# A two-layer recurrence-and-experts kernel: layer 0's router with stationary weights and ScalarE sums of squares, and three shared-expert tiles placed behind the routed experts

## The chip, the cores and the metric

The kernel runs on one core of one Trainium2 chip. Its time is device microseconds of that core, taken over several executions; beside these times there is one execution recorded by the hardware profiler, with a time and a span of its own. All data are f32. The core has a TensorE (matrix products and transposes, with a sequencer for its weight loads), a VectorE, a ScalarE, a GpSimd and a SyncE (SP) that issues most DMAs; PSUM, where TensorE writes, is used here in banks of 128 partitions by 512 f32.

## The reference

`x` and the side input `k` are (4, 512, 512) and `cond` is (4, 128). Two layers are added to `x` one after the other. Each layer runs a recurrence over the tokens and then a mixture of experts on what comes out:

```python
def bi_wkv(r, k, v, w, u, time_emb):              # called with v = k
    tf = sigmoid(sum(time_emb, -1))
    decay = exp(-exp(w)) * (0.5 + 0.5 * tf)
    ek = exp(min(k, 30)); ekv = ek * v
    # a = a*decay + ekv_t, b = b*decay + ek_t, scanned forward (nf, df) and backward (nb, db)
    euk = exp(min(u + k, 30))
    num = nf + nb - ekv + euk * v
    den = df + db - ek + euk
    return sigmoid(r) * (num / max(den, 1e-8)) * (0.8 + 0.2 * tf)

def ffn0(z):          # 8 experts, 2 per token, 256 wide, one shared expert 256 wide
    h = z * rsqrt(mean(z * z) + 1e-6) * rms_weight
    top2 of softmax(h @ router_w), renormalised to sum 1
    return sum_top2 w_e * ((silu(h @ gate_e) * (h @ up_e)) @ down_e) \
           + (silu(h @ sw_gate) * (h @ sw_up)) @ sw_down

def ffn1(z):          # 32 experts, 6 per token, capacity 512, 352 wide, a shared expert 704 wide
    ...

x = x + ffn0(bi_wkv(x, k, k, w0, u0, cond))
x = x + ffn1(bi_wkv(x, k, k, w1, u1, cond))
```

The change concerns `ffn0` alone: the mean of `z * z`, the product with `router_w`, and the shared expert.

## The kernel before, in words

The 2048 tokens are 16 row tiles of 128 (`NT`), in four blocks of four (`NB`, `TB`; a block is one sequence of the batch). The 512 channels are four chunks of 128 (`NC`). Layer 0's recurrence output lies transposed in `zT`: channels on partitions, tokens along the free axis. A unit is one (block, chunk), `zcols(n)` its 128 x 512 part of `zT`; there are 16 units.

**Recurrence.** A loop over n = 0 to 16 works on several units at once, with the order on ScalarE, TensorE and VectorE written out by hand as it stands in the code. In round n TensorE sums the parts of numerator and denominator of unit n-1 (`sums`, L436 and L437, into banks `num` and `den`), ScalarE turns the denominator into a reciprocal with Ln and Exp, `front(n+1)` and `turn(n+3)` prepare later units (`turn` transposes `k`, L394, from `kr`, which SP loads), `mid(n)` holds the scans on VectorE, and `back(n-1)` multiplies the result into `zT`. `sigmoids` (L465) puts sigmoid(x) there first, once for each block.

**Routing of a block.** It runs in the rounds after the block's last unit: `logits0` in the round with chunk 1, then `route_v` (mean square to 1/rms: a VectorE multiply-add, then Ln and Exp on ScalarE), and `route_max`, `route_top`, `route_pay` in the round with chunk 2, `route_pos` and `route_slots` in that with chunk 3. The last block's routing stands behind the loop; I call these four pieces of work the routing quarters (n = 5, 9, 13 and the last). `logits0` holds two groups of 16 products, each product with eight columns of result in bank `pl`: on L481 a 128-token piece of `zT` is the stationary operand and the chunk's `rout` (128 x 8) moves; on L490 a piece of the squared columns is stationary and a column block of ones moves, which sums squares over channels. The squared columns come from `square(n-2)`, one ScalarE activation per unit into one of four buffers with tag `sq`. `row_tile(n-5)` transposes one row tile of `zT` per round back to rows in a bank `tr`, ScalarE copies it to `zr` (L472), and SP stores it to `z0d` in DRAM (L473), from where the routed experts gather their tokens.

**Shared expert of layer 0.** For a row tile t there are six steps: `share_up` (16 products, L579, gate into one half and up into the other half of one PSUM bank `g`), `share_silu` (ScalarE, L584), `share_hid` (VectorE), `share_turn` (two transposes, L596, and a ScalarE copy), `share_down` (two products in four passes, L605) and `share_add` (VectorE adds to the `x` rows in `acc`; SP stores the tile to `xa`, L610). Tiles 0 to 5 are done in pairs inside the loop, at n = 7, 10 and 13. Tiles 6 to 15 follow the last routing quarter as "the tail". `scale_weights` multiplies `rout` and the shared gate and up weights by `rms_weight` on ScalarE (L243) in round 2.

**Routed experts of layer 0.** `routed` walks over eight experts and their slots of 128 tokens, as many as the counts ask for: 35 slots in the profile. For each slot GpSimd gathers 128 rows from `z0d` by an indirect DMA (L763), TensorE transposes them into `pza` (L776), ScalarE copies them with the scale of `rms_weight` to `zgT`, and TensorE makes gate (L826, into bank `pgate0`) and up (L830, into bank `pup0`). ScalarE runs Silu on gate (L833), then `copy_hidden` for the previous slot's transposed hidden row (L795), then scales up (`upt`, L836); GpSimd multiplies both (`hrow`, L837). TensorE makes the down-projection of the previous slot (L804, into one of two banks `pout`), ScalarE copies it (`ob`, L806), and GpSimd adds it by an indirect scatter (L809), in turn to `xa` and to `xb` (which GpSimd set to zero at the start). Weights come from SP in three buffers, `third[0]` being one. VectorE meanwhile does layer 1's recurrence (`wkv1`): 12 units before, four "midway", at e = 2. Its exponentials are made ahead by ScalarE (`exps1_upto`) into free buffers (`spare`).

**Crossing into layer 1.** For each of the 16 tiles SP loads `xa` into `acc` and `xb` into `other`, VectorE adds them (L939), TensorE transposes (L942), ScalarE applies the sigmoid (L944), VectorE multiplies with the recurrence into `zT` (L945), TensorE makes layer 1's router logits (L947, 32 columns, all into one bank `plg`) and transposes back (L952), ScalarE copies `zr` and SP stores `z1d` (L955). The order here is the framework's; where TensorE is free, products of layer 1's shared expert (L1022) stand between. Then layer 1's shared expert runs alone, and then its routed experts, through `routed` with l = 1.

The loop's part that the change touches, as it stands before:

```python
        if n >= 2:
            square(n - 2)
        ...
        turn(n + 3)
        if c == 1 and b >= 1:
            logits0(b - 1)
        for t in pairs0.get(n - 2, ()):
            share_down(t, "g")
        if n >= NC + 1:
            row_tile(n - NC - 1)
```

Of the kernel before, what the change touches and what calls it, by code (L numbers as in the profile page):

```python
# [18 lines left out]
P = 128  # L19
# [11 lines left out]
def adaln_ffn_kernel(  # L31
# [208 lines left out]
    def scale_weights():  # L240
        for c in range(NC):
            for wv in (rout, *shared0[:2]):
                nc.scalar.activation(wv[:, c, :], wv[:, c, :], AF.Copy, scale=rmsw[:, c : c + 1])  # L243

    for tb, width in ((table0, 3), (table1, 2)):
        blank = wk.tile([P, NCOL * width], F32, name=f"blank{width}", tag="sq", bufs=NC)
# [4 lines left out]
    zero = wk.tile([P, D], F32, name="zero", tag="zr")  # L251
# [128 lines left out]
    fronts, mids, squares, routes, pays = {}, {}, {}, {}, {}  # L380
# [73 lines left out]
    def square(n):  # L454
        sq = wk.tile([P, S], F32, tag="sq", name=f"sq{n}", bufs=NC)
        nc.scalar.activation(sq, zcols(n), AF.Square)
        squares[n] = sq

# [8 lines left out]
    def row_tile(t):  # L467
        pz = bank("tr", f"pz{t}")
        for c in range(NC):
            nc.tensor.transpose(pz[:, c * P : (c + 1) * P], zT[:, c, t * P : (t + 1) * P], ident)  # L470
        zr = wk.tile([P, D], F32, tag="zr", name=f"zr{t}")
# [3 lines left out]
    def logits0(b):  # L475

        pl = bank("pl", f"pl{b}")
        for i in range(TB):
            t = b * TB + i
            for c in range(NC):  # L480
                nc.tensor.matmul(  # L481
                    pl[:, i * E0 : (i + 1) * E0],
                    zT[:, c, t * P : (t + 1) * P],
                    rout[:, c, :],
                    start=(c == 0),
                    stop=(c == NC - 1),
                )
        for i in range(TB):
            for c in range(NC):
                nc.tensor.matmul(  # L490
                    pl[:, (TB + i) * E0 : (TB + i + 1) * E0],
                    squares[b * NC + c][:, i * P : (i + 1) * P],
                    ones[:, :E0],
                    start=(c == 0),
                    stop=(c == NC - 1),
                )
        routes[b] = pl


    def route_v(b):  # L500
        pl = routes[b]
        v = wk.tile([P, TB], F32, tag="v", name=f"v{b}")
        ssq = pl[:, TB * E0 : 2 * TB * E0].rearrange("p (i e) -> p i e", e=E0)[:, :, 0]
        nc.vector.tensor_scalar(v, ssq, 1.0 / D, 1e-6, ALU.mult, ALU.add)
# [3 lines left out]
        routes[b] = pl, v, g  # L508

    def route_max(b):  # L510

        pl, v, g = routes[b]
# [58 lines left out]

    shared_up, shared_hid = {}, {}

    def share_up(t):
        gv, uv, _ = shared0
        pgu = bank("g", f"sg{t}")
# [5 lines left out]
    def share_silu(t):  # L582
        sg = wk.tile([P, F0], F32, tag="sg", name=f"ssg{t}")
        nc.scalar.activation(sg, shared_up[t][:, :F0], AF.Silu, scale=rs[:, t : t + 1])  # L584
        shared_up[t] = shared_up[t], sg

    def share_hid(t):
        pgu, sg = shared_up.pop(t)
        hr = wk.tile([P, F0], F32, tag="hr", name=f"shr{t}")
# [3 lines left out]
    def share_turn(t):  # L593
        ph = bank("tr", f"sph{t}")
        for f, _ in CH0:
            nc.tensor.transpose(ph[:, f : f + P], shared_hid[t][:, f : f + P], ident)  # L596
        hT = wk.tile([P, F0], F32, tag="hT", name=f"shT{t}")
# [3 lines left out]
    def share_down(t, tag):  # L601
        dv, hT = shared0[2], shared_hid.pop(t)
        po = bank(tag, f"so{t}")
# [10 lines left out]
    spare = rows[:2] + cols[:4] + rows[2:] + cols[4:]  # L614
# [23 lines left out]
    for n in range(NU + 1):  # L638
# [5 lines left out]
        if n >= 2:  # L644
            square(n - 2)
        if c == 3 and b >= 1:
            route_pos(b - 1)
        if n == 2:
            scale_weights()
        for t in pairs0.get(n - 2, ()):  # L650
            share_turn(t)
        turn(n + 3)
        if c == 1 and b >= 1:
            logits0(b - 1)
        for t in pairs0.get(n - 2, ()):
            share_down(t, "g")
        if n >= NC + 1:
            row_tile(n - NC - 1)
# [31 lines left out]
    square(NU - 1)  # L690
    logits0(NB - 1)
    route_v(NB - 1)
    row_tile(NT - 4)
    row_tile(NT - 3)
    route_max(NB - 1)
    row_tile(NT - 2)
    row_tile(NT - 1)
# [18 lines left out]
    for t in range(early + 2, NT):  # L716
# [6 lines left out]
        if t == 12:  # L723
            exps1_upto(10)
    share_turn(NT - 1)
    for t in (NT - 2, NT - 1):
        share_down(t, "den")
        share_add(t)
    exps1_upto(12)
# [346 lines left out]
```

## Time and profile before

| | before |
|---|---|
| time, median of 3 runs | 1605.63 us (1603.36 to 1611.89) |
| profiled execution: its own time | 1598.96 us |
| its span | 1597.2 us |
| TensorE busy | 1464.5 us, 92% of the span |
| TensorE weight loads (beside the products) | 892.2 us |
| VectorE busy | 682.9 us, 43% |
| GpSimd busy | 579.8 us, 36% |
| ScalarE busy | 399.0 us, 25% |
| granted TensorE clock, mean | 0.956 |
| moved by DMA | 183.40 MB, mean 115 GB/s |

Busy time is that in which an engine executes; waiting and the issuing of DMAs do not count. The granted clock is the share of full speed that TensorE was given; a stretch at 0.5 is one in which every product takes twice its time. In rows of the timeline the columns are the start and the length in us, the engine, the line of the kernel, the operation, result and operands with their shapes, how many instructions are taken together, and in brackets how long the engine waited before it and what ended the wait. An engine that waits off the path costs nothing, so the busy shares of the whole span say little on one stage; they have to be read stage by stage.

### The profile page before, as it was taken

Reading aid. Unit: us, or ns where it says so; the run is one execution under the profiler, and the core shown is the slowest. Engines: PE = TensorE matmul, PEld = TensorE weight load, DVE = VectorE, ACT = ScalarE, POOL = GpSimd, SP = SyncE. Lnnn points to the kernel's source line nnn. Section 1 sums busy time; section 2 is a strip of 40 time slices with the busy share of each in tenths; the row PEclk is TensorE's granted clock in tenths of the full one; section 3 lists DMA queues with packets and bytes.
Section 4 is the critical chain, followed back from the end, with each engine's and each line's share of the span. In section 5 each row is a group of like instructions: output and inputs, shape, how many; then the busy total and the mean of one; then the engine's idle time right before and its main releaser. Section 6 shows DMA issues by size and latency. Waiting matters only on the chain. (4 is left out here: it accounts for less than half of the span.)

```text
span 1597.2 us, 16807 instructions
## 1 busy us (share of the span) xinstructions
PE 1464.5 (92%) x5305; PEld 892.2 (56%) x5305; DVE 682.9 (43%) x1191; ACT 399.0 (25%) x939; POOL 579.8 (36%) x576
## 2 busy tenths in 40 slices
PE   5889989898987739999999999999999999999997
PEld 3556658576655537344444565556555555655654
DVE  6796863699998024461111222222222222222222
ACT  4663442544554315000000111111111111111110
POOL 3010212266666400016663334344333343433332
PEclk9898888999999959999999999999999999999999
DMA  9010001445455365001113654565645585465442
GB/s 351 35 53 27 34 34 65 158 80 111 90 121 132 81 223 175 0 1 37 45 45 108 183 150 128 145 181 157 169 113 136 128 266 120 130 187 132 121 100 41
DMA packets 116251, 183.40 MB, mean 115 GB/s; under 512 B 19912, under 2 KB 63964, under 8 KB 116104
## 3 DMA queue, kind: packets, MB, share of 16 engines
q1 hardware_dynamic: 79192, 120.56, 22.0%
q0 software_dynamic: 36336, 60.04, 19.2%
q8 instruction: 66, 1.08, 0.3%
q10 hardware_dynamic: 576, 1.05, 0.2%
q14 instruction: 81, 0.66, 0.1%
HBM read 149.71 MB, written 52.64 MB: 127 GB/s over the span
## 5 line engine op out<-in xcount | busy, mean ns | idle before, releaser
L804 PE MATMUL pout<-w,hT 128*128 128x512 f32 (+1 forms) x432 | 203.0, 603 | 1.3 <-DVE hT L797 0.8
L826 PE MATMUL pgate<-w,zgT 128*128 128x352 f32 (+1 forms) x656 | 191.7, 436 | 7.9 <-PEq L883 5.5
L830 PE MATMUL pup<-w,zgT 128*128 128x352 f32 (+1 forms) x656 | 188.3, 430 | 0.0
L809 POOL DMA_INDIRECT out_dram<-ob,put x52 | 82.6, 1589 | 281.3 <-DVE ob L808 143.2
L763 POOL DMA_INDIRECT acc<-z1d,put x119 | 123.0, 1033 | 137.2 <-PE pza L776 60.4
L353 POOL DMA_INDIRECT table<-pay,r1sloti x96 | 93.2, 971 | 187.8 <-DVE hid L1025 161.2
L842 DVE SCALAR_TENSOR_TENSOR hrow<-pup,tab,sgt 128x352 f32<-128x352 f32 x84 | 49.1, 584 | 255.7 <-issue 131.6
L826 PEld LDWEIGHTS pgate<-w,zgT 128*128 128x128 f32 x656 | 121.8, 193 | 63.3 <-issue 10.8
L830 PEld LDWEIGHTS pup<-w,zgT 128*128 128x128 f32 x656 | 122.4, 190 | 48.7
L808 DVE COPY ob<-pout 128x512 f32<-128x512 f32 x84 | 58.1, 692 | 174.4 <-PE pout L804 164.7
L804 PEld LDWEIGHTS pout<-w,hT 128*128 128x128 f32 (+1 forms) x432 | 77.5, 193 | 68.6 <-issue 54.7
L353 POOL DMA_INDIRECT table<-r0pay,r0sloti x32 | 35.3, 1103 | 210.9 <-DVE r0sloti L343 158.2
L776 PEld LDWEIGHTS pza<-ident,acc 128*128 128x128 f32 x584 | 71.7, 141 | 60.3 <-issue 27.5
L776 PE MATMUL pza<-ident,acc 128*128 128x128 f32 x584 | 87.9, 276 | 17.6 <-DMA acc<-z0d,put 14.3
L799 ACT COPY hT<-phT 96x128 f32<-96x128 f32 x84 | 21.9, 261 | 287.4 <-DVE hT L797 282.4
L786 ACT COPY zgT<-pza 128x256 f32<-128x256 f32 x103 | 38.3, 372 | 209.5 <-DVE zgT L785 154.1
L1031 PE MATMUL o<-w,hid 128*128 128x512 f32 (+1 forms) x192 | 86.0, 603 | 2.7 <-DVE acc L1034 2.2
L804 PE MATMUL pout<-zT,hT 128*128 128x512 f32 (+1 forms) x192 | 87.8, 592 | 0.0
L1022 PE MATMUL u<-zT,w 128*128 128x512 f32 (+1 forms) x192 | 86.8, 592 | 0.0
L1022 PE MATMUL g<-zT,w 128*128 128x512 f32 (+1 forms) x192 | 86.3, 592 | 0.0
L790 PE MATMUL phT<-ident,hrow 128*96 128x128 f32 (+1 forms) x322 | 55.8, 276 | 30.3 <-DVEq L883 15.2
L826 PE MATMUL pgate<-zT,zgT 128*128 128x352 f32 x256 | 81.0, 459 | 0.0
(261 smaller groups left out, 2205.7 us busy)
## 6 DMA issues: line engine op xcount, KB each, us to landing
w<-in_L_ffn_w_dram SPq DMA_DIRECT2D x44, 704.0 KB
zT<-in_L_ffn_w_dram SPq DMA_DIRECT2D x20, 704.0 KB
w<-in_L_ffn_w_dram SPq DMA_DIRECT2D x22, 512.0 KB
zT<-in_L_ffn_w_dram SPq DMA_DIRECT2D x10, 512.0 KB
w<-in_L_ffn_w_dram SPq DMA_DIRECT2D x22, 192.0 KB
acc<-in_x_dram SPq DMA_DIRECT2D x4, 1024.0 KB
xb<-zero POOLq DMA_DIRECT2D x16, 256.0 KB
z0d<-zr SPq DMA_DIRECT2D x16, 256.0 KB
```

Source lines behind the costliest of these rows:

```text
L353: ins = nc.gpsimd.indirect_dma_start(out=table, out_offset=bass.IndirectOffsetOnAxis(ap=sloti[:, t, j : j + 1], axis=0), in_=pay[:, t, j, ...
L763: nc.gpsimd.indirect_dma_start(out=rows(e, s), out_offset=None, in_=zd, in_offset=bass.IndirectOffsetOnAxis(ap=put_at[:, e * NS + s : e * ...
L776: nc.tensor.transpose(pza[which][:, c * P : (c + 1) * P], rows(e, s)[:, c * P : (c + 1) * P], ident)
L790: nc.tensor.transpose(phT[:m, j * P : (j + 1) * P], hrow[:, f : f + m], ident)
L804: nc.tensor.matmul(po, hT[:m, j, :], dv[:m, j, :], start=(j == 0), stop=(j == nf - 1))
L808: nc.vector.tensor_copy(row, po)
L809: nc.gpsimd.indirect_dma_start(out=outs[n % len(outs)], out_offset=bass.IndirectOffsetOnAxis(ap=at, axis=0), in_=row, in_offset=None, boun ...
L826: nc.tensor.matmul(pg, zt[:, c, :], gv[:, c, :], start=(c == 0), stop=(c == NC - 1))
L830: nc.tensor.matmul(pu, zt[:, c, :], uv[:, c, :], start=(c == 0), stop=(c == NC - 1))
L842: nc.vector.scalar_tensor_tensor(hrow, pu, tab[:, col, 1:2], sgt, ALU.mult, ALU.mult)
L1022: nc.tensor.matmul(p[:m], wv[:, c, f : f + m], zT[:, c, cols], start=(c == 0), stop=(c == NC - 1))
L1031: nc.tensor.matmul(po, hid[:m, j, i * P : (i + 1) * P], dv[:m, j, :], start=(j == 0), stop=(j == len(FCH) - 1))
```

## The change

In layer 0's router `rout` becomes the stationary operand: four products over 512 tokens each give the logits of a block transposed (8 x 512). ScalarE copies them to `lgT`, and one round later `turn_logits` transposes them back to the form that the routing reads. The sums of squares no longer come from products with ones: `row_turn` transposes a row tile, and a ScalarE Square on that PSUM bank sums along the row (`accum_out`) into `ssq`. `row_out` then copies and stores the rows. All four row tiles of a block now stand in the round with chunk 1, with `logits0` between the second and the third; `zr` has four buffers instead of two, `sq` has one, and `square` is gone. The two blank tables written at the start share one buffer instead of having one each.

Tiles 13 to 15 of the shared expert leave the tail. `xa` is filled for them from `x` by a DMA at the start, and their expert output is made behind the last routed slot, into three PSUM banks `late13` to `late15`; their hidden steps use the routed stage's banks `pza` and `phT`. For this the shared weights are loaded a second time (at e = 6, into `third[0]`) and scaled again (at e = 7). The crossing begins with tiles 13 to 15, and for these VectorE adds the late bank as well.

Beside the three late banks, the routed stage of layer 0 now has gate and up in the two halves of one bank `pgu0`, and one `pout` bank instead of two. The crossing has fewer banks too; its logits are copied from `plg` to `lg1` at its end, and layer 1's shared expert opens its banks after that.

Of layer 1's recurrence 10 units instead of 12 come before the routed experts, the other six at e = 1 instead of four at e = 2; the exponentials are split in the same way.

```diff
-    def scale_weights():
+    def scale_weights(*weights):
         for c in range(NC):
-            for wv in (rout, *shared0[:2]):
+            for wv in weights:
                 nc.scalar.activation(wv[:, c, :], wv[:, c, :], AF.Copy, scale=rmsw[:, c : c + 1])
     for tb, width in ((table0, 3), (table1, 2)):
-        blank = wk.tile([P, NCOL * width], F32, name=f"blank{width}", tag="sq", bufs=NC)
+        blank = wk.tile([P, NCOL * width], F32, name=f"blank{width}", tag="lgT", bufs=1)
...
-    zero = wk.tile([P, D], F32, name="zero", tag="zr")
+    zero = wk.tile([P, D], F32, name="zero", tag="zr", bufs=TB)
...
-    def square(n):
-        sq = wk.tile([P, S], F32, tag="sq", name=f"sq{n}", bufs=NC)
-        nc.scalar.activation(sq, zcols(n), AF.Square)
-        squares[n] = sq
...
-    def row_tile(t):
-        pz = bank("tr", f"pz{t}")
+    def row_turn(t, tag="tr"):
+        b, i = divmod(t, TB)
+        if i == 0:
+            ssq[b] = wk.tile([P, TB], F32, tag="ssq", name=f"ssq{b}")
+        pz = bank(tag, f"pz{t}")
         for c in range(NC):
             nc.tensor.transpose(pz[:, c * P : (c + 1) * P], zT[:, c, t * P : (t + 1) * P], ident)
-        zr = wk.tile([P, D], F32, tag="zr", name=f"zr{t}")
+        sq = wk.tile([P, D], F32, tag="sq", name=f"sq{t}", bufs=1)
+        nc.scalar.activation(sq, pz, AF.Square, accum_out=ssq[b][:, i : i + 1])
+        return t, pz
+
+    def row_out(t, pz):
+        zr = wk.tile([P, D], F32, tag="zr", name=f"zr{t}", bufs=TB)
         nc.scalar.copy(zr, pz)
         nc.sync.dma_start(z0d[t * P : (t + 1) * P, :], zr)
     def logits0(b):
         pl = bank("pl", f"pl{b}")
+        for c in range(NC):
+            nc.tensor.matmul(pl[:E0], rout[:, c, :], zcols(b * NC + c), start=(c == 0), stop=(c == NC - 1))
+        lgT = wk.tile([E0, S], F32, tag="lgT", name=f"lgT{b}", bufs=1)
+        nc.scalar.copy(lgT, pl[:E0])
+        routes[b] = lgT
+
+    def turn_logits(b):
+        pl = bank("pl", f"plt{b}")
         for i in range(TB):
-            t = b * TB + i
-            for c in range(NC):
-                nc.tensor.matmul(pl[:, i * E0 : (i + 1) * E0], zT[:, c, t * P : (t + 1) * P], rout[:, c, :], ...)
-        for i in range(TB):
-            for c in range(NC):
-                nc.tensor.matmul(pl[:, (TB + i) * E0 : (TB + i + 1) * E0],
-                    squares[b * NC + c][:, i * P : (i + 1) * P], ones[:, :E0], ...)
+            nc.tensor.transpose(pl[:, i * E0 : (i + 1) * E0], routes[b][:, i * P : (i + 1) * P], ident[:E0, :E0])
         routes[b] = pl
     def route_v(b):
-        ssq = pl[:, TB * E0 : 2 * TB * E0].rearrange("p (i e) -> p i e", e=E0)[:, :, 0]
-        nc.vector.tensor_scalar(v, ssq, 1.0 / D, 1e-6, ALU.mult, ALU.add)
+        nc.vector.tensor_scalar(v, ssq[b], 1.0 / D, 1e-6, ALU.mult, ALU.add)
...
+    LATE = NT - 3
+    nc.sync.dma_start(xa[LATE * P :, :], xf[LATE * P :, :])
...
+        if c == 2 and b >= 1:
+            turn_logits(b - 1)
         if c == 1 and b >= 1:
-            logits0(b - 1)
+            for t in range((b - 1) * TB, b * TB):
+                row_out(*row_turn(t))
+                if t % TB == 1:
+                    logits0(b - 1)
         for t in pairs0.get(n - 2, ()):
             share_down(t, "g")
-        if n >= NC + 1:
-            row_tile(n - NC - 1)
...
-    square(NU - 1)
+    pz = [row_turn(t, "den" if t % 2 else "tr") for t in range(NT - TB, NT)]
     logits0(NB - 1)
     route_v(NB - 1)
-    row_tile(NT - 4)
-    row_tile(NT - 3)
+    row_out(*pz[0])
+    row_out(*pz[1])
+    turn_logits(NB - 1)
     route_max(NB - 1)
-    row_tile(NT - 2)
-    row_tile(NT - 1)
+    row_out(*pz[2])
+    row_out(*pz[3])
...
-    for t in range(early + 2, NT):
+    for t in range(early + 2, LATE):
...
-        if t == 12:
-            exps1_upto(10)
+        if t == 10:
+            exps1_upto(8)
...
-    exps1_upto(12)
+    exps1_upto(10)
...
-        pg = px.tile([P, F], F32, name=f"pgate{l}")
-        pu = px.tile([P, F], F32, name=f"pup{l}")
-        pout = [px.tile([P, D], F32, name=f"pout{l}{h}") for h in range(2)]
+        if l == 0:
+            pgu = px.tile([P, 2 * F], F32, name="pgu0")
+            pg, pu = pgu[:, :F], pgu[:, F:]
+        else:
+            ...
+        pout = [px.tile([P, D], F32, name=f"pout{l}{h}") for h in range(1 + l)]
...
-            if e == 2 and midway is not None:
-                midway()
+            if e in extra:
+                extra[e]()
...
+    late_out = [late_ps.tile([P, D], F32, name=f"late{t}") for t in range(LATE, NT)]
...
+        def shared_again():
+            nonlocal shared0
+            shared0 = put_weights(third[0], sw_gate, sw_up, sw_down)
+
...
+                {1: wkv1_rest, E0 - 2: shared_again, E0 - 1: lambda: scale_weights(*shared0[:2])},
...
+            spool = rp
+            for t in range(LATE, NT):
+                share_up(t, pza[t % 2])
+                share_silu(t)
+                share_hid(t)
+                if t > LATE:
+                    share_turn(t - 1, phT)
+                    share_down(t - 1, po=late_out[t - 1 - LATE])
+            share_turn(NT - 1, phT)
+            share_down(NT - 1, po=late_out[NT - 1 - LATE])
...
-        for t in range(NT):
+        late = list(range(LATE, NT))
+        for t in late + list(range(LATE)):
...
             nc.vector.tensor_tensor(acc[:, t, :], acc[:, t, :], other, ALU.add)
+            if t >= LATE:
+                nc.vector.tensor_tensor(acc[:, t, :], late_out[t - LATE], acc[:, t, :], ALU.add)
...
+    lg1 = rt.tile([P, NT, E1], F32, name="lg1")
+    nc.vector.tensor_copy(lg1, plg.rearrange("p (t e) -> p t e", e=E1))
+    psz.close()
+    latep.close()
+    ...
+    banks.update(pool=ps, tr=0, g=2, u=2, o=2)
...
-        pr, key = yield from softmax(plg.rearrange("p (t e) -> p t e", e=E1), NT, E1, rt, "r1")
+        pr, key = yield from softmax(lg1, NT, E1, rt, "r1")
```

## The prediction

> **What bounds the kernel now.** I read the busy time by stage first (my own stretches, TensorE, weight load, VectorE, ScalarE, GpSimd, then granted clock, DMA share, GB/s), then each engine's timeline in the stretches that the diff touches, then who waited for whom. The chain that ended last was of no use: it reaches back only to 1569 us, inside layer 1's experts.
>
> ```profile
> 34.40:231.00 196.60, 177.84 (x667) 114.45 (x668) 155.70 (x328) 100.69 (x176) 23.68 (x20) 0.86 0.13 47
> 231.00:253.00 22.00, 22.00 (x116) 20.65 (x115) 6.91 (x43) 6.24 (x12) 3.87 (x4) 0.69 0.16 60
> 253.00:301.00 48.00, 46.85 (x187) 33.19 (x185) 15.67 (x39) 19.04 (x36) 11.75 (x13) 1.00 0.21 71
> 301.00:564.00 263.00, 223.93 (x942) 158.57 (x942) 210.82 (x213) 119.83 (x358) 158.58 (x117) 0.95 0.49 113
> 564.00:586.40 22.40, 0.02 (x1) 0.03 (x1) 0.77 (x2) 0.54 (x1) 1.57 (x1) 0.57 0.80 258
> 586.40:601.00 14.60, 13.36 (x64) 12.96 (x64) 7.89 (x13) 6.16 (x10) 0.00 (x0) 0.50 0.48 172
> 601.00:627.00 26.00, 25.93 (x205) 22.73 (x205) 11.81 (x19) 12.33 (x23) 0.00 (x0) 0.99 0.67 233
> ```
>
> The stages are the recurrence with three routing quarters, the last routing quarter, the shared tail, the routed experts, a hole, and the crossing into layer 1 (two lines). TensorE sets the pace nearly everywhere, except in the hole (22.4 us, TensorE 0.02) and in parts of the recurrence, where VectorE alternates with it. Two stretches run far below full clock: 0.69 in the routing quarter, 0.50 at the start of the crossing.
>
> **Routing quarters (about -24 us).** One quarter of routing, in TensorE's and VectorE's timelines:
>
> ```profile
> 119.94 3.64 PE L481 MATMUL pl<-rout,zT 128*128 128x8 f32 x32
> 123.43 6.96 PE L490 MATMUL pl<-ones,sq 128*128 128x8 f32 x32
> 130.24 5.39 PE L605 MATMUL so<-w,shT 128*128 128x512 f32 x8
> 130.42 0.16 DVE L504 TENSOR_SCALAR v<-pl 128x4 f32<-128x4 f32 x1 [4.59 <-PE pl L490]
> 136.28 0.42 DVE L406 TENSOR_SCALAR ek<-kA 128x512 f32<-128x512 f32 x1
> ```
>
> The same 32 passes cost 0.11 us each on L481 and 0.22 on L490: eight-column products let the clock fall to half, and the next two down-projections (5.39) still pay for it; undisturbed they took 3.60 us at 171.51. VectorE has nothing to do and waits. The change takes out both groups and puts in 4 products of 512 columns. One such product (two passes) advances TensorE by 0.86 us (L436 to L437), so 3.44 us; four tiny transposes back come to about 0.45. The four row turns (0.43 each) only move here from four iterations. ScalarE keeps 16 squares and 16 row copies (about 0.5 us apart), and gains one 8x512 copy a quarter, taken as 0.5. The accumulating square is in no row: as the plain one at the low end, 0.2 more at the high end; I take the plain one.
>
> How much reaches the path I followed by hand, quarter by quarter.
> - First (n=5): TensorE would free itself at 74.5 instead of 80.24, but VectorE now waits for the fourth sum of squares, at about 76.1 after four squares and copies in ScalarE's queue, where it went on at 79.62. The layer's next unit and the whole routing of the quarter queue behind that wait. Gain 3.5.
> - Second (n=9): TensorE reaches the next sums at 128.95 instead of 135.91. The two Silus behind it, and the exp of the softmax in their queue, come as much earlier. Gain 7.0.
> - Third (n=13): the sums start at 192.2 instead of 199.93; `lg` now waits for the transposed logits, which stand behind these sums in TensorE's queue, and gives 0.8 back. Gain 6.9.
> - Last (231 to 253): root and logits wait for 3.44 us of products instead of 11; the softmax's exp comes at 240.6 instead of 246.42, and tile 8's up-projection at 246.2 instead of 252.90. Gain 6.7.
>
> Sum 24.1. If VectorE takes over everywhere, each is worth 3.5: 14.
>
> **The first load (+2 us).**
>
> ```profile
> 34.41 1.09 PE L394 MATMUL pk<-ident,kr 128*128 128x128 f32 x4 [5.91 <-DMA kr<-in_fside_BxSxS_dram]
> ```
>
> TensorE waits here for kr1, with the DMA engines 0.95 busy at 345 GB/s. The change puts a copy of 768 KB from x to xa directly ahead of kr1 in SP's queue: 786,432 bytes at this stage's 390 GB/s is 2.0 us. Bounds: 0, if it only takes room from x's later blocks; 4, if a DRAM-to-DRAM byte counts twice. I take 2. GpSimd's zero stores are interleaved with the two blank tables, which now share a buffer; the same bytes go out before 20 us, so nothing.
>
> **Three tail tiles moved (-16.2 us).**
>
> ```profile
> 263.69 3.62 PE L579 MATMUL sg<-w,zT 128*128 128x256 f32 x16
> 267.14 0.38 PE L596 MATMUL sph<-ident,shr 128*128 128x128 f32 x2
> 267.36 1.88 PE L605 MATMUL so<-w,shT 128*128 128x512 f32 x4
> 269.08 3.62 PE L579 MATMUL sg<-w,zT 128*128 128x256 f32 x16
> ```
>
> A tile costs 269.08 - 263.69 = 5.39 us and TensorE never waits, so three take 16.2 us from the path. The routed stage can follow: GpSimd's table read hangs on the route, which came 6 us earlier, and gather 1 on tile 8. Gathers 2 and 3 wait for tile 11's store to xa, which is now the tail's last but one: they stand behind it in GpSimd's queue and land about 2 us late, mostly under the hidden row's wait of 1.16 at 310.08; I charge 0.5. Three stores of 256 KB leave SP's queue. The tail drops four exps on ScalarE, where nothing waits.
>
> **What the three tiles cost later.** In front of the crossing TensorE ends L804 at 563.6 and next works at 586.38, after the scatters' landing, 16 issues for xa and the first xb tile:
>
> ```profile
> 560.15 3.77 PE L804 MATMUL pout<-w,hT 128*128 128x512 f32 x4 [0.52 <-ACT hT L795]
> 585.63 3.10 DVE L939 TENSOR_TENSOR acc<-acc,other 128x512 f32<-128x512 f32 x5 [73.77 <-DMA other<-xb]
> 586.38 1.97 PE L942 MATMUL pt<-ident,acc 128*128 128x128 f32 x8 [22.45 <-DVE acc L939]
> ```
>
> Three tiles at 5.39, plus three short waits for the hidden copy (0.7 each) and 1 us at half clock, end near 583. They fit: 0. If that cover went they would cost all 16. VectorE adds the first late tile before the first transpose, +0.7. At the crossing's end the logits are copied (0.6) before layer 1's banks open, +0.5. The layer-1 products that filled TensorE in the crossing (5 x 0.86 = 4.3 us) move behind it, one for one.
>
> Loading the shared weights again is three DMAs of 512 KB on SP's queue at e=6, where no other load is due; no scatter is queued behind SP there. Scaling them is 8 activations at 0.445 (L243, 0.89 for two) = 3.5 us of ScalarE; the exps inside the routed stage go from 8 to 12 (+0.53 each). Against the 2.7 us that ScalarE has idle in a slot, these come to +0.5 and +1.3.
>
> **One bank for gate and up (+16 us).** This is the cost that the title does not name. `pgate0` and `pup0` become halves of one bank `pgu0`. In the changed kernel's instruction order the Silu still waits for TensorE, but the scaling of up no longer does: the Silu's wait now covers both. Before:
>
> ```profile
> 539.02 1.89 PE L826 MATMUL pgate<-w,zgT 128*128 128x256 f32 x8
> 541.01 0.47 ACT L833 ACTIVATE sgt<-pgate,tab 128x256 f32<-128x256 f32 x1 [1.11 <-PE pgate L826]
> 542.96 0.47 ACT L836 ACTIVATE upt<-pup,tab 128x256 f32<-128x256 f32 x1 [1.21 <-PE pup L830]
> 543.13 1.88 PE L804 MATMUL pout<-w,hT 128*128 128x512 f32 x4
> 256.56 0.47 ACT L584 ACTIVATE ssg<-sg,rs 128x256 f32<-128x256 f32 x1 [3.08 <-PE sg L579]
> ```
>
> The last line is the tail, where both halves do share a bank: the Silu starts 3.66 us after the first product (252.90), behind both. In a routed slot it starts 1.99 us after. The Trainium skill's "PSUM — Partial Sum Buffer", in Terms, says that TensorE writing and ScalarE reading one bank at once collide; by that the wait is there in every slot, and without it the sum would be 16 us better. The tail's row is on its side, and I follow it.
>
> Its price: the Silu moves from 1.99 to 3.94 after the gate's start, the hidden copy behind it ends at 4.67, and the down-projection, which waits for that copy, starts at 4.83 instead of 4.11: +0.72. ScalarE's four turned copies then end at 6.14, before TensorE is free at 6.55, so the period goes from 5.83 to 6.55. Of 35 slots, the first has no down-projection; seven first slots of an expert turn two tiles before it, +0.29; ten wait 0.15 to 3.55 us for a gather just there and hide part, 1.8 in all; 17 pay in full, 12.2. Sum 16. Bounds 8 (more hidden under gathers) and 26 (35 x 0.72). With `pout` on one bank nothing waits: its copy ends 3 us before the next.
>
> **Sum.** -24.1 +2.0 -16.2 +0.5 +0.7 +0.5 +1.8 +16.0 = -18.8 us. The profiled execution took 1598.96 us for a span of 1597.2, and lies 0.4% under the median of 1605.63. I take the difference off the median: 1587 us. About 0.5%, 8 us, is what a measurement of this kernel can tell from no change.
>
> **The clock, by row and by rule.** The crossing starts at 0.50 for 14.6 us though TensorE is 91% busy, and is then at 0.99 for transposes and 32-column products alone (601.67 to 607). The Trainium skill's "TensorE: Matmul & The Clock Gate" says in Part 4 that transposes do not count as busy, and in "Why this matters for your kernels" that a gap over about 3 us drops the clock. A gap of 3 us or more stays ahead of the first transpose (583 to 587), so I give the late tiles no credit for a warm start (about 5 us, if they had it). By Part 4 taken strictly the crossing, without its wide fillers, would stay at half: 16 tiles at 3.42 are 55 us against 36 of own work before, +19, and the sum 0. The trace's 0.99 stretch speaks against that.
>
> **Rivals.**
> - The bank wait hides: the slots are bound by gathers and branches, and only the gains are left, -35, 1571 us. For: 14 us of gather waits. Against: 17 slots with no wait at all. 0.12.
> - VectorE takes over: quarters worth 14 instead of 24, or the bank wait 26: -9, 1597 us. For: n=5 goes that way already. 0.20.
> - Slower: the clock stays at half from the last scatter to the end of the crossing. Late tiles take 34.5 us and end near 600, 14 us past their cover, and the crossing 19 more: +33 - 18.8, 1620 us. It decides from 27 us on, so it needs both. For: the 0.57 and 0.50 rows. Against: dense 256-column products came up within 5 us (247.5 to 252). 0.06.
> - The sum as it stands, 1578 to 1596: 0.62.
>
> Faster by over 0.5%: 0.58 of the main case, the first rival and half of the second, 0.80. Slower: 0.05. Within: 0.15. The range, 1571 to 1603, takes in the first two rivals and leaves out the clock.
>
> **What would show it.** L490 gone, and 3.4 us of 8x512 products in its place at full clock; VectorE's wait at the root ended by ScalarE. Five tail tiles at 5.39. Silu waiting for up in layer 0's slots, with the period near 6.5 us; if it stays at 5.8, the bank step is wrong. The late tiles inside the hole, ending before the first xb tile lands. pk waiting for kr1 to about 36.5. The sum fails above all if the slot period is over 7 us or the crossing stays at half clock.

## The result, and the profile after

The changed kernel takes 1601.37 us (median of 20 runs, 1593.03 to 1606.95); the kernel before took 1606.65 us in as many runs beside it. The ratio of the means is 0.9961, interval 0.9944 to 0.9977: 6.3 us faster (3.7 to 9.0), a third of the 18.8 us forecast. The shorter tail is worth what it was costed at and the router nearly so; the routed stage behind them gives more back than was put.

The stages of the changed kernel, in the columns of the prediction's first table (stretch, its length, TensorE, weight load, VectorE, ScalarE, GpSimd busy, granted clock, DMA share, GB/s):

```profile
0.00:35.70 35.70, 15.65 (x50) 9.39 (x50) 24.41 (x44) 15.79 (x27) 13.18 (x36) 0.93 0.96 346
35.70:211.60 175.90, 154.54 (x505) 81.89 (x506) 151.76 (x324) 101.68 (x188) 22.90 (x19) 0.94 0.15 55
211.60:228.20 16.60, 14.22 (x70) 9.69 (x69) 7.46 (x38) 8.37 (x20) 5.33 (x5) 1.00 0.18 65
228.20:261.90 33.70, 32.48 (x123) 22.53 (x121) 12.17 (x36) 14.69 (x26) 9.78 (x11) 0.95 0.18 62
261.90:557.40 295.50, 239.89 (x943) 165.86 (x944) 206.10 (x213) 120.57 (x369) 172.26 (x119) 0.92 0.47 108
557.40:577.20 19.80, 18.06 (x67) 12.51 (x65) 2.11 (x4) 2.91 (x7) 1.57 (x1) 0.95 0.71 225
577.20:581.90 4.70, 0.05 (x1) 0.00 (x0) 1.48 (x3) 0.00 (x0) 0.00 (x0) 0.79 0.71 209
581.90:600.20 18.30, 17.27 (x80) 16.13 (x81) 10.57 (x18) 7.47 (x12) 0.00 (x0) 0.50 0.53 191
600.20:625.30 25.10, 20.17 (x179) 18.92 (x177) 10.70 (x20) 11.56 (x22) 0.00 (x0) 0.98 0.73 245
```

The last routing quarter is now 16.6 us at full clock (third line), the tail 33.7 us, and the hole of 22.4 us has become 19.8 us of late tiles and 4.7 us of waiting. The fifth line is the loss: the routed experts take 295.5 us instead of 263.

One trace of each kernel is a poor measure here. I took the kernel before twice more and the changed one once more (experiments e5 to e7). Stage by stage, in us; the routed stage runs from the first gate product to the start of its last down-projection:

| stage | before, three traces | after, two traces | difference of means | forecast |
|---|---|---|---|---|
| start to the first routed gate | 302.4, 295.9, 300.1 | 263.1, 264.8 | -35.4 | -38.3 |
| routed experts, layer 0 | 257.8, 270.5, 258.3 | 290.6, 289.9 | +28.1 | +18.3 |
| to the first transpose of the crossing | 26.2, 25.2, 25.0 | 28.2, 28.3 | +2.7 | +0.7 |
| crossing and layer 1's shared expert, to the first transpose of layer 1's routed experts | 291.2, 297.9, 297.8 | 296.3, 296.5 | +0.8 | +0.5 |
| layer 1's routed experts | 719.6, 719.5, 719.2 | 721.8, 721.6 | +2.2 | 0 |

The sum is -1.6 us on these five traces and -6.3 us in the runs. I put the difference down to the spread of the traces, which is not shown: the same kernel's routed stage differs by 12.7 us and its crossing by 6.6 us from trace to trace. The execution on which the prediction rests was 7.7 us under the later median, and the +2.2 of the last row is gone in e9 and e10, which have the same code there (719.1 and 719.4).

The changed quarter, then the first load, in TensorE's and VectorE's timelines:

```profile
118.07 3.60 PE L483 MATMUL pl<-zT,rout 128*8 128x512 f32 x8
121.60 1.09 PE L469 MATMUL pz<-ident,zT 128*128 128x128 f32 x8
122.53 3.60 PE L608 MATMUL so<-w,shT 128*128 128x512 f32 x8
124.14 0.17 DVE L501 TENSOR_SCALAR v<-ssq 128x4 f32<-128x4 f32 x1 [1.59 <-ACT sq L471]
...
35.69 1.09 PE L394 MATMUL pk<-ident,kr 128*128 128x128 f32 x4 [8.02 <-DMA kr<-in_fside_BxSxS_dram]
```

Four products of 512 columns (eight passes) stand where two groups of 32 eight-column passes stood. The granted clock, 0.50 from 123.5 to 133.7 in before, is 1.00 here (118 to 126), and the down-projections behind the products take 3.60 us instead of 5.39. VectorE's wait, 1.59 us instead of 4.59, is now ended by ScalarE's square. `kr1`, the second unit's `kr`, comes at 35.69 instead of 34.41.

### The profile page after: what moved, and what is told of

Same layout as the page of the kernel before. It is cut to its first block, busy times and chain, and to the rows that moved or that the text cites. A ratio compares the mean times of both kernels' runs of the same rounds, so it can differ in the third digit from the quotient of the medians.

```text
span 1600.1 us, 16354 instructions
## 1 busy us (share of the span) xinstructions
PE 1458.0 (91%) x5097; PEld 860.8 (54%) x5097; DVE 678.1 (42%) x1192; ACT 399.9 (25%) x966; POOL 593.0 (37%) x576
## 3 DMA queue, kind: packets, MB, share of 16 engines
q0 software_dynamic: 36336, 60.04, 19.8%
## 5 line engine op out<-in xcount | busy, mean ns | idle before, releaser
L813 PE MATMUL pout<-w,hT 128*128 128x512 f32 (+1 forms) x432 | 206.9, 612 | 10.6 <-ACT hT L804 9.3
L835 PE MATMUL pgate<-w,zgT 128*128 128x352 f32 x416 | 133.2, 463 | 0.1
L839 PE MATMUL pup<-w,zgT 128*128 128x352 f32 x416 | 131.5, 459 | 0.0
L839 PEld LDWEIGHTS pup<-w,zgT 128*128 128x128 f32 x416 | 79.0, 190 | 44.0
L835 PEld LDWEIGHTS pgate<-w,zgT 128*128 128x128 f32 x416 | 75.8, 192 | 34.0 <-issue 1.2
L795 ACT COPY zgT<-pza 128x256 f32<-128x256 f32 x103 | 38.3, 373 | 210.3 <-DVE zgT L794 158.7
L839 PE MATMUL pup<-zT,zgT 128*128 128x352 f32 x256 | 81.0, 459 | 0.0
```

Of the source, the lines that this page charges most:

```text
L795: nc.scalar.copy(dst[:, h:, :], pza[which][:, h * P :].rearrange("p (c t) -> p c t", c=h))
L813: nc.tensor.matmul(po, hT[:m, j, :], dv[:m, j, :], start=(j == 0), stop=(j == nf - 1))
L835: nc.tensor.matmul(pg, zt[:, c, :], gv[:, c, :], start=(c == 0), stop=(c == NC - 1))
L839: nc.tensor.matmul(pu, zt[:, c, :], uv[:, c, :], start=(c == 0), stop=(c == NC - 1))
```

## The experiments

Ratios are to the kernel before in the same runs, and times that are gained or lost are worked out from them. For e11 and e12 the plain medians give less: 39.6 us where the ratio gives 43, and 18.5 where it gives 21.

### The two parts alone: e1, e12 and e2

e1 and e12 are one kernel, before with the router part only (`row_turn`, `row_out`, `logits0`, `turn_logits`, `ssq`).

> The kernel before with the router part alone (stationary router weights, ScalarE sums of squares, row turns in one round); the tail, the routed stage and the crossing are those of before. The traces of before and after put the router's gain at 23 us when the shared tail begins (tile 8's up-projection at 228.2 instead of 252.9, less 1.7 us at half clock in it). Theory A, the gain stays: 23 us faster than before, ratio 0.986. Rival, the routed stage behind it waits for gathers or for GpSimd's table and takes half back: 10 us faster, ratio 0.994.

> The router part alone once more, for a narrower interval of its worth and a second trace. By the traces it brings the first routed gate from 299.4 us (mean of three traces of before) to 280.9, so 18.5 us. If the time follows, ratio 0.9885; if the routed stage behind it gives a part back, as its first measurement of 0.992 with an interval from 0.989 to 0.995 may mean, 0.992 again.

Measured: 0.9919 (0.9887 to 0.9951) and 0.9869 (0.9822 to 0.9917): 13 and 21 us, 17 in the mean. In their traces the first routed gate comes at 280.9 and 277.1 us, 20.4 us before the mean of the three traces of before. The forecast was 24.1 for this part. The routed stage in them was 273.9 and 267.1 us, against a mean of 262.2 before; their waits at the ends of experts summed to 20.1 and 20.6 us. So the gain is there, and perhaps some us of it are lost behind; the intervals do not settle how many, and theory A's 23 us is outside e1's.

e2 is before with one bank for gate and up, and one `pout`:

```diff
-        pg = px.tile([P, F], F32, name=f"pgate{l}")
-        pu = px.tile([P, F], F32, name=f"pup{l}")
-        pout = [px.tile([P, D], F32, name=f"pout{l}{h}") for h in range(2)]
+        pgu = px.tile([P, 2 * F], F32, name="pgu0")        # l == 0
+        pg, pu = pgu[:, :F], pgu[:, F:]
+        pout = [px.tile([P, D], F32, name=f"pout{l}{h}") for h in range(1 + l)]
```

> The kernel before with one edit alone: gate and up of layer 0's routed stage in the two halves of one PSUM bank, and one bank for pout. Theory A, the bank is what lengthens the routed stage: Silu waits for up in all slots, the slot period goes from 5.83 to 6.57 us, TensorE's stage grows by 20 to 28 us, more than the 16 of the prediction; ratio 1.013 to 1.018. Theory B, the prediction's sum: 16 us, ratio 1.010. Rival C, the stage is longer in the changed kernel because of the second load and scaling of the shared weights, and the bank costs under 10 us, ratio under 1.006.

Measured: 1.0111 (1.0067 to 1.0154), 17.8 us slower; routed stage 279.1 us, 16.9 over the mean of before. The forecast of 16 stands (theory B), the interval reaches into theory A's range (from 1.013), rival C falls. A slot in its timeline, TensorE and then ScalarE:

```profile
346.38 1.98 PE L808 MATMUL pout<-w,hT 128*128 128x512 f32 x4 [0.34 <-ACT hT L799]
348.21 1.89 PE L830 MATMUL pgu<-w,zgT 128*128 128x256 f32 x8
349.93 0.38 PE L794 MATMUL phT<-ident,hrow 128*128 128x128 f32 x2
350.15 1.89 PE L834 MATMUL pgu<-w,zgT 128*128 128x256 f32 x8
351.98 0.66 PE L780 MATMUL pza<-ident,acc 128*128 128x128 f32 x4
352.95 1.98 PE L808 MATMUL pout<-w,hT 128*128 128x512 f32 x4 [0.31 <-ACT hT L799]
...
345.60 0.47 ACT L837 ACTIVATE sgt<-pgu,tab 128x256 f32<-128x256 f32 x1 [3.08 <-PE pgu L834]
```

Period 6.57 us, forecast 6.55; the Silu waits for up (L834), in 33 of the 35 slots. The edit changes `pout` too, but in the profile the down-projection waits only for `hT`, never for the copy of the bank. The step was right in mechanism and size. But 17.8 is not the 28.1 of the stage table: about 10 us of the changed kernel's routed stage are not the bank.

### Where the other ten are: e9 and e10

The length of single experts places them. From the first gate to the second expert's gate: 73.6 us in e2, but 79.4 and 79.5 in the two traces after. From there to the third: 60.0 in e2, 64.4 and 64.8 after. From there to the last down-projection: 145.5 in e2, 146.9 and 145.6 after. So nearly all of it lies in the first two experts, 5.9 and 4.6 us, and the second load and scaling of the weights at the end add at most 0.8 us in the mean.

First expert. GpSimd's first three gathers in before, then in after:

```profile
272.95 1.06 POOL L763 DMA_INDIRECT acc<-z0d,put  x1 [2.50 <-DMA xa<-acc]
292.70 1.00 POOL L763 DMA_INDIRECT acc<-z0d,put  x1 [18.69 <-DMA xa<-acc]
294.01 1.00 POOL L763 DMA_INDIRECT acc<-z0d,put  x1 [0.31 <-issue]
```

```profile
250.01 1.06 POOL L772 DMA_INDIRECT acc<-z0d,put  x1 [3.49 <-DVE zT L915]
262.44 1.95 POOL L772 DMA_INDIRECT acc<-z0d,put  x1 [11.36 <-DVE v L916]
264.69 1.92 POOL L772 DMA_INDIRECT acc<-z0d,put  x1 [0.30 <-DVE v L264]
```

TensorE where it turns the gathered rows, in before (first line) and in after:

```profile
305.87 1.04 PE L776 MATMUL pza<-ident,acc 128*128 128x128 f32 x8
270.11 1.12 PE L785 MATMUL pza<-ident,acc 128*128 128x128 f32 x4 [3.28 <-DMA acc<-z0d,put]
271.85 1.12 PE L785 MATMUL pza<-ident,acc 128*128 128x128 f32 x4 [0.63 <-DMA acc<-z0d,put]
272.76 3.56 PE L835 MATMUL pgu<-w,zgT 128*128 128x256 f32 x8
```

Before, the second gather was issued 9.65 us ahead of the first gate (302.35); after, 0.69 us ahead of it (263.13). It goes into tile 11's row of `acc`, which the tail must first add to and store. Tile 11 is now the tail's last but one: VectorE adds it at 258.96, where TensorE ends the tail at 260.64, and SP issues its store at 259.68. The profile names VectorE for the end of GpSimd's wait; that it is this store is read from the buffers. The two gathers then also take 7.6 and 7.1 us to land, beside the weight loads that SP issues from 260.67 on; in e9, below, they land in 3.6 and 3.5. TensorE waits 3.28 and 0.63 us, and the gate product behind runs at half clock (3.56 instead of 1.97). e9 gives the first three gathers the rows of tiles 13, 14 and 15, which the tail no longer touches:

```diff
-        zg = [acc[:, NT // 2 + h, :] for h in range(8)]
+        zg = [acc[:, t, :] for t in ((13, 15, 12, 14, 8, 10, 11, 9) if l == 0 else range(8, 16))]
```

> The changed kernel with one edit: the gathers' buffers of layer 0's routed stage are handed out in another order, so that the first three gathers go into the rows of tiles 13 to 15 (which the tail no longer uses) instead of rows of tiles that the tail is still adding to. In the traces of the changed kernel the second and third gather are issued 0.7 us before the first gate product, in before 9.7 us before it, and the first expert takes 5.9 us longer than in the kernel with the shared bank alone. Theory A: these gathers cost it; with the edit the first expert is 4 to 6 us shorter, ratio to before 0.993. The prediction's reading (0.5 us, hidden under the hidden row): no change, 0.996.

Measured: 0.9931 (0.9904 to 0.9958), 4.8 us less than the changed kernel. The gathers are issued before 250, TensorE turns their rows without a wait, and the first expert takes 73.7 us again, as in e2:

```profile
247.26 1.11 POOL L772 DMA_INDIRECT acc<-z0d,put  x1 [0.82 <-POOL put L718]
248.68 1.00 POOL L772 DMA_INDIRECT acc<-z0d,put  x1 [0.30 <-DVE zT L915]
249.99 1.00 POOL L772 DMA_INDIRECT acc<-z0d,put  x1 [0.30 <-PE sph L598]
...
266.66 1.04 PE L785 MATMUL pza<-ident,acc 128*128 128x128 f32 x8
```

The intervals of 0.9931 and 0.9961 overlap; the expert's length (79.4, 79.5, and 79.4 in e3, against 73.7) is the stronger evidence.

Second expert. The block of exponentials on ScalarE and the down-projection behind it, in before (at e = 2) and then in after (at e = 1):

```profile
435.75 1.28 ACT L624 ACT_TABLE_LOAD   x1
...
441.70 1.28 ACT L917 ACT_TABLE_LOAD   x1
...
443.78 2.23 PE L804 MATMUL pout<-third,hT 128*128 128x512 f32 x4
```

```profile
350.40 1.28 ACT L627 ACT_TABLE_LOAD   x1
...
358.61 1.28 ACT L929 ACT_TABLE_LOAD   x1
359.91 0.47 ACT L842 ACTIVATE sgt<-pgu,tab 128x256 f32<-128x256 f32 x1
360.28 0.36 ACT L804 COPY hT<-phT 128x256 f32<-128x256 f32 x1
...
360.70 3.78 PE L813 MATMUL pout<-w,hT 128*128 128x512 f32 x4 [2.67 <-ACT hT L804]
```

Eight exponentials between two table loads (the rows ACT_TABLE_LOAD) held ScalarE for 7.2 us, and the down-projection did not wait for the hidden copy. Twelve hold it for 9.5 us; the Silu and the hidden copy queue behind them, TensorE waits 2.67 us and then runs a down-projection at half clock. e10 makes four of the twelve ahead of the first slot:

```diff
     exps1_upto(10)
-    nc.scalar.preload_act_table_set("silu_and_others")
     order.close()
...
         for n in range(10):
             wkv1(n)
+        exps1_upto(12)
+        nc.scalar.preload_act_table_set("silu_and_others")
```

> The changed kernel with one edit: four of the twelve layer-1 exponentials that stand at e = 1 are made just ahead of the first routed slot, so that eight stay there as in before. Theory A: twelve exponentials and two table loads hold ScalarE for 9.5 us and TensorE waits 2.7 us for the hidden copy and then runs at half clock; with eight this wait is under 1 us: the routed stage is 4 us shorter, less up to 2 us that the four cost ahead of the first slot; ratio to before 0.994. The prediction's reading (1.3 us for these and the scaling): 1 us, 0.9955.

Measured: 0.9922 (0.9891 to 0.9954), 6.2 us less than the changed kernel (the intervals just overlap). The second expert takes 61.0 us instead of 64.4 and 64.8, and the first gate comes at 263.86, no later. TensorE's wait for the hidden copy is gone there, but it waits 3.31 us for a gather in its place, so of the 6.2 us only 3.6 are placed.

Added up, e9 and e10 are 11.0 us in time and 9.3 in the length of the two experts, against 12.5 us that the forecast missed. No run has both edits in the changed kernel; in the version of e11 below, the two together gave 7.5 us.

### The crossing: e3

lg1 gets memory that exists since the start (it also takes the unused squares and one exponential) instead of the pool `rt`, which opens behind the crossing.

> The changed kernel with lg1 in memory of its own instead of the pool that follows the crossing (the unused square goes to the same tile, and so does one exponential of layer 1). Theory A: the copy of the logits stood behind the last stores of z1d, whose memory the pool takes over; without that it starts within 1 us of the last transpose, the 4.2 us gap goes to about 1, and the first layer-1 product runs at full clock (3.6 instead of 6.6 us): 6 us faster than the changed kernel, ratio to before about 0.992. Rival: the banks' release, not the pool, holds it, and the gap stays: no difference from the changed kernel, 0.996.

Measured: 0.9969 (0.9948 to 0.9991), no faster than the changed kernel. The end of the crossing there (VectorE, TensorE), and then in e3 (VectorE, then TensorE):

```profile
624.55 0.69 DVE L991 COPY lg<-plg 128x512 f32<-128x512 f32 x1 [5.08 <-DMA z1d<-zr]
625.29 6.57 PE L1060 MATMUL g<-zT,w 128*128 128x512 f32 x8 [4.22 <-DVE lg L991]
```

```profile
622.58 0.69 DVE L992 COPY lg<-plg 128x512 f32<-128x512 f32 x1 [1.17 <-PE plg L980]
625.95 0.69 DVE L286 TENSOR_REDUCE r1mx<-lg 128x16 f32<-128x512 f32 x1 [2.68 <-DMA z1d<-zr]
...
623.73 3.70 PE L1061 MATMUL g<-zT,w 128*128 128x512 f32 x8 [0.72 <-ACT zr L987]
649.01 10.56 PE L1070 MATMUL o<-w,hid 96*128 96x512 f32 x20 [2.70 <-DVE hid L1064]
```

The reading of the wait was right: the gap is 0.72 instead of 4.22 us and the product has full clock. But VectorE then waits for the same last stores at its next operation; the softmax starts at 625.95 instead of 625.29, and TensorE waits 2.70 us for a hidden product of VectorE instead, with a slow stretch behind it (20 products in 10.56 us). The two stages together went from 296.4 to 294.8 us. A wait in front of a queue had only been moved along it; the copy itself takes 0.69 us.

### Without the shared bank: e4, e8 and e11

The shared bank exists because three late banks are held until the crossing. e4 copies each late result to SBUF at once, so that the routed stage and the crossing have their old banks:

```diff
+            def late_down(t):
+                po = pout[t % 2]
+                share_down(t, po=po)
+                nc.vector.tensor_copy(late_out[t - LATE], po)      # ob[0..2], in a pool opened ahead of r0
```

> The changed kernel with gate, up and pout in the banks of the kernel before: the three late tiles' results are copied from a pout bank to SBUF by VectorE at once, so no bank is held, and the crossing has before's banks, with no copy of the logits. Theory A: the router (-23) and the tail (-16) remain, the late tiles give 2 to 4 back, the second load and scaling 2 to 5: 30 us faster than before, ratio 0.981. Rival C, the second load and scaling and the late tiles' place are what lengthened the routed stage: it stays near 290 us, and the kernel is 12 us faster than before, ratio 0.992.

Measured: 0.9879 (0.9838 to 0.992), 19.4 us faster than before, between the two expectations. The routed stage was 265.7 us, so rival C falls again; but the crossing began 36.0 us after the last routed down-projection:

```profile
561.24 0.69 PE L598 MATMUL phT<-ident,shr 128*128 128x128 f32 x2 [10.87 <-DVE shr L591]
```

In VectorE's order additions of the crossing, which wait for `xb`, stood ahead of the last late tile's product. e8 makes the additions come after it:

```diff
+            tc.add_manual_dep(added, late_last.name, after, reason="late tiles first")
```

> The version with the late tiles' results in SBUF, with one dependency more: VectorE's first additions of the crossing come after the last late tile. In the version before this, VectorE's order put two additions, which wait for the loads of xb, ahead of the last late tile's hidden product; TensorE waited 10.9 us for it, and the crossing began 36.0 us after the last routed down-projection instead of 26.2. Theory A: without that it begins 26 to 28 us after it, and the kernel is 8 us faster than that version, ratio to before 0.983. Rival: the loads of xa and xb set the start, the wait of TensorE was beside them: no change, ratio 0.988.

Measured: 0.9777 (0.9737 to 0.9817), 35 us faster than before; the crossing begins 26.8 us after the last down-projection. That is 16 us better than e4 where 8 were expected: 9.2 are the earlier start of the crossing, the rest is within the two intervals. e11 adds the edits of e9 and e10:

> The version with the late tiles' results in SBUF and the added dependency, with both edits: the gathers' buffers in the other order, and four exponentials ahead of the first routed slot. Theory A: 5 to 8 us faster than that version (ratio to before 0.9777), ratio 0.973 to 0.975. Rival: in that version, without the shared bank, both costs lie under waits that are there anyway: no change, 0.978.

Measured: 0.973 (0.9685 to 0.9774), median 1565.85 us, 43 us faster than before and the fastest version here. Its first expert takes 66.6 us, where e8 had 73.7. By the ratios this is 7.5 us better than e8, though the two intervals overlap; the rival's 0.978 lies just outside e11's.

### Traces again: e5, e6, e7

No edit; each is one execution.

> The kernel before once more, for its trace. In the trace of before TensorE waited 9.8 us in all at the seven ends of an expert, and the crossing ran at half clock for 15 us; in the five other traces these waits were 15 to 20 us, and the router alone, whose code from the tail on is that of before, had 20.2 us and 29 us. Theory A, chance of the execution: a second trace of before has 15 to 20 us there too, and a routed stage (first gate to last down-projection) of 266 to 274 us instead of 257.8. Theory D, the changed kernels' earlier start of the stage causes the longer waits: before again has 10 us and 258 us.

> The kernel before a third time, for its trace, with the same two expectations: by A waits of 15 to 20 us at the ends of experts and a stage of 266 to 274 us, by D 10 us and 258 us.

> The changed kernel once more, for its trace. The slot period with gate and up in one bank is fixed by the order of waits: 6.57 us in the slots that wait for nothing else, in this trace too. The waits at the ends of experts were 17.7 us; by theory A (chance of the execution) they may lie anywhere from 10 to 20, by D at 17 to 18. The gap ahead of layer 1's first shared product is 4.2 us again if the last stores of z1d set it.

The waits at the ends of experts were 14.5 and 14.4 us in before, between A and D, with stages of 270.5 and 258.3 us: inconclusive. In e7 they were 17.1 us, the slot period was 6.57 again and the gap ahead of layer 1's first shared product 4.16. Over all traces the waits run from 8.7 to 20.6 us; the two router traces have the highest. An early start of the stage (theory D) does not by itself set them: e2 starts it at 301.9 and has 17.0, e11 at 266.5 and has 8.7. The DMA records hold a trail that no run followed: in 82 of the 98 ends (seven in each of 14 traces) a packet of an instruction queue (q8) starts 2.5 to 3.7 us ahead of the next expert's first gate product. That TensorE waits there for instructions is not shown. What sets the waits stays open, and with it some 7 us (20.4 in the two router traces against a mean of 12.9 in before).

## Why the prediction was wrong, by its own steps

- **Quarters, -24.1.** Right in kind, too high: 20.4 us on the traces, about 17 in time. Up to the last round's sums the two router traces are 16.5 us ahead of the mean of before, where the first three quarters were put at 17.4. The last quarter gives 3.9 where 6.7 was put, but from these sums to tile 9's up-projection the three traces of before differ by 5.8 us among themselves. The fourth sum of squares of the first quarter was put at 76.1; VectorE's operation starts at 76.25 in after, but that is with the later first load, and at 75.05 and 74.15 in the router traces.
- **First load, +2.0.** Right: `kr1` comes 1.5 us later than in the three traces of before on average (35.7 against 34.2), and in the recurrence's last sums the two traces of after are 2.6 us behind the two router traces, which have no copy (203.0 against 200.4 in the mean).
- **Tail, -16.2.** Right to the tenth: 23.0 us were gained at tile 9's up-projection and 39.2 at the first gate of the same two traces.
- **Gathers, +0.5.** This step failed. The prediction saw that gathers 2 and 3 stand behind tile 11, "now the tail's last but one", and put them about 2 us late, mostly under another wait. They lost 9 us of lead, because the down-projections of the tail's last two tiles stand together at its end, these tiles are now 11 and 12, and tile 11's add waits for its own; in the old tail that add (288.17) lay 14 us ahead of the first gate. Price 5.7 us of expert length, 4.8 in time.
- **ScalarE's blocks, +1.8.** Failed in size. The block of exponentials was set against the idle time of an average slot; it is one block of 9.5 us with two table loads, and what waits behind it is the hidden copy. Four more exponentials cost 3.4 us or more of the second expert, 6.2 in time by e10, where 1.3 was put. The reload and scaling are nearly free.
- **One bank, +16.** Right: 17.8 (10.7 to 24.7) alone, period 6.57 for 6.55. The Trainium skill's "PSUM — Partial Sum Buffer", in Terms, says that TensorE writing and ScalarE reading one bank at once collide; no run here shows a collision. What the runs show is that the Silu waits for up.
- **Late tiles, 0, and the add, +0.7.** They ran inside the hole, and ended at 577.24, but the crossing started 2.7 us later than the hole had ended before. SP's queue shows it, in before, in after and in e8:

```profile
570.05 9.36 SPq L936 DMA_DIRECT2D acc<-xa  x16
579.79 8.08 SPq L938 DMA_DIRECT2D other<-xb  x11
```

```profile
563.47 9.56 SPq L965 DMA_DIRECT2D acc<-xa  x16
577.38 8.37 SPq L967 DMA_DIRECT2D other<-xb  x13
```

```profile
545.96 9.33 SPq L968 DMA_DIRECT2D acc<-xa  x16
555.72 12.51 SPq L970 DMA_DIRECT2D other<-xb  x14
```

  In after the 16 loads of `xa` are issued by 573.0, and the first load of `xb` only at 577.38, as soon as TensorE ends the last late product: `other` lies where the routed stage's pool lay, and that pool is held by the late tiles. In e8, where the weights and hidden rows of the late tiles lie in a pool of their own, `xb` follows `xa` with no such gap. That share was argued from the queue; no run changed it alone.
- **Logits copy, +0.5.** The row of the table came out at +0.8, but by luck. The three traces of before are of two kinds there (last section); against the one on which the prediction rests the changed kernel is 5.2 us longer. Part of that is the wait of 4.22 us and the product at half clock behind it (6.57 instead of 3.70), which the prediction did not have; e3 took both away and won 1.6 us of the stage.
- **The rivals.** The clock's rival fell: the late tiles ran at 0.95, and 18.3 us of half clock at the start of the crossing lie within what the kernel before shows, and from 600.2 on the crossing was granted 0.98. The bank wait did not hide. VectorE did not take over in the quarters.
- **The time.** The forecast missed by 12.5 us. By the stage table the routed stage is 9.8 us over its forecast: 5.2 from the gathers (5.7 where 0.5 was put) and 2.3 or more from the exponentials (3.6 where 1.3 was put), both placed by e9 and e10; the bank is 0.9 over by the stage (16.9), and some 1.4 us are not placed. The late tiles are 2.0 over, and the quarters up to 7, with a wide interval. The median of 1601.37 us lay inside the stated range of 1571 to 1603, but near its slow end and for another reason than the second rival's, and the kernel before was 1 us slower than assumed; two small terms had been read off averages.

## What to carry to other kernels

When work is shortened ahead of a stage, follow the stage's first inputs back to the buffer that is released last, and ask which tile now releases it: a gather that had 9 us of lead lost it to a tile two places from the end, and another order of buffers gave it back. A block on a queue is to be weighed whole, with its table loads, against the one wait behind it, not against the idle time of an average slot. And before PSUM banks are shared to hold a result, look for a copy on an idle engine: here three copies to SBUF took the place of a shared bank that cost 17.8 us.

## What the runs showed of the hardware that was not expected

- An accumulating square is two instructions on ScalarE: the activation, and a read of the accumulator that shows 0.20 us but moves the next operation by only 0.10 us:

```profile
69.44 0.60 ACT L471 ACTIVATE sq<-pz 128x512 f32<-128x512 f32 x1
69.93 0.20 ACT L471 ACTIVATION_READ_ACCUMULATOR sq<-pz 128x1 f32 x1
70.03 0.59 ACT L476 COPY zr<-pz 128x512 f32<-128x512 f32 x1
```

- The clock of the crossing took one of two courses in the same code. In three traces (before, e2, e12) it was granted 0.50 for the first 15 us and the stage took 291.2 to 291.6 us; in three others (e1, e5, e6) it was 0.50 for 29 us and the stage took 297.8 to 297.9. What decides is not known. Such a row of one trace is no baseline for a change of a few us.
